# A 3x3 convolution inside a fused network: nine taps, or minimal filtering over pairs of columns

## The chip, the cores and the metric

The kernel runs as one program on one core of a Trainium2 chip. The metric is the device time of one execution in microseconds (us). Engines are named as the profile names them: PE (TensorE matmul), PEld (TensorE weight load), DVE (VectorE), ACT (ScalarE), POOL (GpSimd) and SP (SyncE, which here only issues DMAs). The time before the change is 3184.22 us, the median of three runs (3183.93 to 3184.84).

## The reference

The input is `x`, two images of 128 channels and 56 x 56 pixels in float32. Four layers follow, each added to `x` after a normalization of its input: agent attention (L0), a 3x3 convolution with 128 channels in and out (L1), a mixture of 8 experts over 2x2 patches with the two best experts for each patch (L2), and a two-way state space scan over rows (L3). The reference writes the convolution with Fourier transforms; what it computes is

```python
PAD = 1
xp = jnp.pad(x, ...)                       # one pixel of zeros on every side
out = sum over i, j of weight[:, :, i, j] applied to xp[:, :, i : i + 56, j : j + 56]
return out + bias[None, :, None, None]
```

which is nine products of a 128 x 128 matrix with shifted pictures.

## The kernel before, in words

`layers` (line 1864) runs the four layers in order. Channels lie on the 128 partitions and pixels on the free axis; an image of 3136 pixels is worked on in seven blocks of 448 columns (8 rows), `BLK`, `NBLK` and `ROWS`. `x` stays in SBUF for the whole kernel, and each layer adds its result to it in place. After each such addition `take_stats` (line 84) takes the statistics of the block, and `group_norm` (line 90) later turns the seven into mean and inverse deviation, which takes two tiny matmuls and two ACT operations. `normed` (line 109) applies them.

**Attention.** `short_attention` (line 384) goes through 14 blocks (7 of each image), each in 25 steps. In every step, `score` (line 574) makes scores on PE and exponentials on ACT and sums them on DVE (lines 592 and 594), and `average` (line 596) multiplies an earlier step's exponentials with the values. The exponentials have five buffers. The order of PE, ACT and DVE is written out by hand there (`manual_schedule`, line 732); POOL is not among these engines and is ordered by the framework's planner, which works with its own estimates of cost. At set steps the loop also runs a piece of other work: the pieces that close the block before (`after`, line 720: divide, project, measure, root, normalize, turn_back, restat), those that prepare the next one (`ahead`, line 729), and at the free steps whatever stands in the list `rest`: first image 0's last values, the preparation of the convolution's weights (`taps`, line 441) and the opening of image 1. POOL does two things here: the softmax scaling of `a_e` (line 549) and the addition of a finished block to `x` (line 687).

**Convolution of image 0.** It is begun in the attention. From the last but one block on (line 744), `rest` holds the norm of image 0 and seven calls of `pad` (line 846), which write normalized rows into a picture with a border of zeros, 58 x 58, in the buffer that held image 0's normalized input. After the last block, at line 784, the seven closing pieces of that block alternate with seven calls of `block` (line 864): nine matmuls of 448 columns into one PSUM bank, one for each tap, then one DVE operation that adds bias and result to `x` (line 876), then the statistics. A check of the softmax's ranges follows (lines 793 to 812); its one number `wide` decides at the end of the kernel whether everything is done again with `agent_attention`. In the profile it isn't.

**Convolution of image 1.** It lies in the routing of the experts. `route` (line 900) calls `convolved` (line 1879) for each image; image 0 is already done, and for image 1 it takes the norm, pads the whole picture with `pad` on DVE into a buffer of the experts' weights (tag `w1`), and then gives out one block at a time. After the second block the router's work for image 0, `patches(0)` (line 962), is issued; after the last one, that for image 1. Then follow the routing tables, the gathers, and the experts. At the same time `MambaWeights` (line 1300) loads the weights of the last layer through ACT's DMA queue and turns them with PE and DVE. In this part the planner orders all engines.

**Weights.** `loads` (line 828) fetches the 128 x 128 x 9 weights and turns them with nine PE transposes in three calls of `turn`, each followed by one ACT copy into `wt`.

[...]in the attention three pairs for scores and passing work (tag `sc`) and two single ones; in the convolution of image 1 four banks for its sums (tag `conv`).

## Time and profile before

| what | us |
|---|---|
| median of the three timed runs | 3184.22 |
| the profiled execution's own time | 3175.44 |
| its span, first to last instruction | 3173.7 |
| attention ends (last softmax sums on PE) | about 902 |
| convolution of image 0 on PE | 901.9 to 953.0 |
| range check, norm of image 1 | 953.0 to 963.5 |
| convolution of image 1 on PE, with image 0's router work | 964.1 to 1019.6 |
| routing | 1020 to 1068 |
| experts | 1068 to 1749 |
| last layer | 1749 to 3174 |

One execution was profiled, so all durations below come from it; the median is of other executions. A row of a stretch gives its length and the busy time of each engine in it, with the count of instructions in brackets. A row of the timeline gives start, length, engine, line, operation and how many like instructions were merged; what stands in square brackets is the idle time of the engine ahead of it and what ended it. A row of a tile or a line gives the least, median and greatest duration in nanoseconds. A float32 matmul leaves two records, so counts of matmul records are twice the counts in the code.

### The profile page before, as it was taken

How to read it: one execution, taken by the hardware profiler on the slowest of the kernel's cores; microseconds unless marked ns; L12 is line 12 of the kernel's file. 1: busy time of each engine (PE TensorE's matmuls, PEld its weight loads, DVE VectorE, ACT ScalarE, POOL GpSimd, SP SyncE). 2: the span in 40 equal slices, each digit the busy share in tenths (PEclk: the TensorE clock that was granted, in tenths of full speed). 3: DMA queues.
4: the chain of work that ended last, by engine and by line, in shares of the span. 5: the costliest groups of instructions: out<-in, count | busy, mean ns of one | idle time of the engine just before them, and what ended most of it. 6: DMA issues, size and time to landing. Idle time of an engine off the chain costs nothing. (4 is left out here: it accounts for less than half of the span.)

```text
span 3173.7 us, 34586 instructions
## 1 busy us (share of the span) xinstructions
PE 2863.2 (90%) x13024; PEld 1091.1 (34%) x13024; DVE 2201.9 (69%) x1985; ACT 1752.3 (55%) x2618; POOL 1411.1 (44%) x755
## 2 busy tenths in 40 slices
PE   7899999998999799999995689998898988999985
PEld 3233333332344444444442223332233332233321
DVE  5788999998854211111112389999999999999997
ACT  5678878887720111111100367777777777777764
POOL 2000010000000000000002389999999999999996
PEclk9999999999998899999997698998999999898987
DMA  1000000000001687878755434454444354445350
GB/s 53 1 1 1 1 1 1 1 1 1 1 31 27 266 323 283 324 282 322 286 228 178 103 72 95 88 104 89 92 87 101 84 107 89 85 87 108 81 111 7
DMA packets 133397, 333.65 MB, mean 105 GB/s; under 512 B 20100, under 2 KB 90596, under 8 KB 129620
## 3 DMA queue, kind: packets, MB, share of 16 engines
q1 hardware_dynamic: 111616, 304.87, 33.5%
q0 software_dynamic: 5136, 14.70, 1.4%
q10 hardware_dynamic: 16452, 11.61, 1.1%
q8 instruction: 107, 1.75, 0.2%
q14 instruction: 86, 0.70, 0.1%
HBM read 262.56 MB, written 17.20 MB: 88 GB/s over the span
## 5 line engine op out<-in xcount | busy, mean ns | idle before, releaser
L1667 POOL TENSOR_TENSOR dBu<-dtu,Bs 128x896 f32<-128x896 f32 x448 | 923.2, 2087 | 72.2 <-DVE h L1689 52.2
L1689 DVE TENSOR_TENSOR_SCAN h<-dA,dBu 128x896 f32<-128x896 f32 x448 | 878.6, 2006 | 58.1 <-ACT dA L1656 56.5
L587 ACT ACTIVATE ex<-sc 128x896 f32<-128x896 f32 (+1 forms) x700 | 602.8, 917 | 111.1 <-PE sc L584 99.9
L594 DVE TENSOR_TENSOR ex_sum<-ex_sum,ex 128x1792 f32<-128x1792 f32 (+1 forms) x238 | 490.0, 2059 | 44.1 <-ACT ex L587 30.0
L1709 PE MATMUL y<-h,both 128*64 128x448 f32 x1792 | 474.5, 631 | 15.6 <-POOL h L1695 13.0
L584 PE MATMUL sc<-q,k 32*128 32x448 f32 (+1 forms) x2800 | 403.0, 589 | 3.6 <-ACT ex L587 2.9
L1208 PE MATMUL h_ps<-w,xs_c 128*128 128x512 f32 x896 | 392.0, 595 | 10.6 <-issue 9.9
L1656 ACT ACTIVATE dA<-dt,f_A 128x448 f32<-128x448 f32 x448 | 284.4, 637 | 110.3 <-DVE h L1689 76.8
L602 PE MATMUL av<-ex,va 128*32 128x448 f32 (+1 forms) x2800 | 335.0, 553 | 0.1
L1698 DVE TENSOR_TENSOR h<-h,c_ps 128x1792 f32<-128x1792 f32 x154 | 311.3, 2022 | 25.6 <-PE c_ps L1677 10.8
L549 POOL TENSOR_TENSOR a_e<-a_e,a_inv 112x784 f32<-112x784 f32 x14 | 41.6, 2973 | 644.1 <-ACT ex L587 436.5
L1656 ACT ACTIVATE dA<-dt,b_A 128x448 f32<-128x448 f32 x448 | 283.7, 636 | 62.9 <-DVE h L1689 50.0
L1212 DVE TENSOR_TENSOR he<-h_ps,sg 128x512 f32<-128x512 f32 x56 | 38.6, 691 | 397.0 <-PE h_ps L1208 374.3
L1159 POOL DMA_INDIRECT xr<-xd,whom x28 | 28.0, 998 | 593.8 <-PE xr_ps L1198 489.2
L1695 POOL TENSOR_TENSOR h<-h,Cs 128x1792 f32<-128x1792 f32 x70 | 279.1, 3986 | 3.2 <-DVE h L1689 2.8
L1677 PE MATMUL c_ps<-low,ident 40*64 40x448 f32 x616 | 173.2, 643 | 91.4 <-DVE h L1698 69.3
L1208 PEld LDWEIGHTS h_ps<-w,xs_c 128*128 128x128 f32 x896 | 168.5, 190 | 218.6 <-issue 201.9
L1709 PEld LDWEIGHTS y<-h,both 128*64 128x64 f32 x1792 | 117.9, 152 | 319.9 <-issue 248.4
L584 PEld LDWEIGHTS sc<-q,k 32*128 32x128 f32 (+1 forms) x2800 | 137.4, 181 | 231.1 <-issue 134.8
L1229 PE MATMUL o_ps<-w,ht 128*128 128x512 f32 x448 | 200.0, 599 | 8.0 <-DMA w<-in_L_conv_w_dram 8.0
L1231 ACT ACTIVATE ot<-o_ps,share 128x512 f32<-128x512 f32 x28 | 19.2, 688 | 287.0 <-PE o_ps L1229 287.0
L1211 ACT ACTIVATE sg<-h_ps 128x512 f32<-128x512 f32 x56 | 33.4, 597 | 256.8 <-PE h_ps L1208 256.8
(318 smaller groups left out, 3007.1 us busy)
## 6 DMA issues: line engine op xcount, KB each, us to landing
w<-in_L_conv_w_dram SPq DMA_DIRECT2D x28, 4096.0 KB, 19.5
w<-in_L_conv_w_dram SPq DMA_DIRECT2D x28, 2048.0 KB, 10.3
Bs<-far SPq DMA_DIRECT2D x56, 896.0 KB, 10.7
dtu<-sp_u SPq DMA_DIRECT2D x112, 224.0 KB, 3.9
dt<-dt SPq DMA_DIRECT2D x112, 224.0 KB, 5.2
Cs<-far SPq DMA_DIRECT2D x140, 112.0 KB, 7.5
os<-ot ACTq DMA_DIRECT2D x28, 256.0 KB, 7.8
xd<-xt SPq DMA_DIRECT2D x14, 224.0 KB, 2.8
```

Of the source, the lines that this page charges most:

```text
L584: nc.tensor.matmul(sc[:size, j, :BLK], self.m.k[rows, at : at + size], self.q[rows, :], start=True, stop=True)
L587: nc.scalar.activation(ex[:size, 2 * g : 2 * g + 2, :], sc[:size, :, :BLK], AF.Exp, scale=scale)
L594: nc.vector.tensor_add(self.total[g][:size], self.total[g][:size], ex[:size])
L602: nc.tensor.matmul(self.av[rows, :BLK], self.m.va[:size, i, rows], self.ex[i][:size, h, :], start=i == 0, stop=i == STEPS - 1,)
L1208: nc.tensor.matmul(h_ps, xc[:, q, :], w1[:, q, f0 : f0 + 512], start=q == 0, stop=q == 3)
L1229: nc.tensor.matmul(o_ps, ht[:, i, :], w2[:, i, :], start=i == 0, stop=i == nj - 1)
L1656: nc.scalar.activation(self.dA[u][:, r * BLK : (r + 1) * BLK], self.dt2[:, m, r, :], AF.Exp, scale=self.w.A[:, j, 2 * m + r : 2 * m + r + 1],)
L1667: nc.gpsimd.tensor_tensor(self.dBu[u], self.dtu2[:, m], self.B[:, j, :].unsqueeze(1).to_broadcast(shape), ALU.mult)
L1689: nc.vector.tensor_tensor_scan(hf, af, bf, 0.0, ALU.mult, ALU.add)
L1695: nc.gpsimd.tensor_tensor(h4, h4, c, ALU.mult)
L1698: nc.vector.tensor_tensor(h4, h4, c, ALU.mult)
L1709: nc.tensor.matmul(self.y[r * H : (r + 1) * H, m, :BLK], both, self.hc[j][:, m, r, :], start=False, stop=j == PAIRS - 1)
```

## The change

Two neighbouring outputs of a row need four neighbouring padded columns d0, d1, d2, d3. With the taps k0, k1, k2 of a row of the filter the change forms four products in place of six: k0 (d0 - d2), (k0 + k1 + k2)/2 (d1 + d2), (k0 - k1 + k2)/2 (d2 - d1) and k2 (d1 - d3). The first output is the first product plus the second plus the third; the second output is the second minus the third minus the fourth. Summed over the three rows of the filter this is twelve products for each pair of columns, each over half as many columns.

- `loads` keeps nine transposes, now grouped by column of the filter, three to a copy, and gets a fourth stage, `mix`, of four POOL operations that forms the two mixed sets. `wt` grows from 9 to 12 matrices.
- `pad` becomes `planes`: the normalized rows go into a small scratch buffer with two places (8 rows of 58 each), and four two-input operations over every second column write four planes of 28 columns. For image 0, inside the attention, these run on POOL; for image 1 on DVE. The planes of image 0 lie in the former buffers of its input and its keys (`xn0`, `k0`), the scratch in that of its values (`va0`); those of image 1 in a `w1` and a `w2` buffer of the experts.
- `block` becomes `group`: 16 rows at a time (three groups, and one of 8 rows), in halves. `left` makes products 1 and 2 (six matmuls into two banks), adds the first to the even columns of `x` on DVE, and copies the second, with bias, to SBUF on ACT. `right` makes products 3 and 4, copies the third with ACT, and subtracts the fourth from the odd columns on DVE. `rest` forms difference and sum of the two copies on POOL, adds them on DVE and takes the statistics of the group's blocks. A group's `rest` is issued behind the next group's `left`.
- In the tail of the attention the seven closing pieces alternate with eight half groups. In the routing, `patches(0)` is issued after the first group in place of the second block. The sums have two pairs of banks in place of four single ones.

```diff
-                    pad = one.tile([P, PAD * PAD], F32, name="pad0", tag="xn0")
+                    planes = [
+                        one.tile([P, PAD * PAD], F32, name=f"planes{i}", tag=tag)[:, : PAD * HW].rearrange(
+                            "c (i h w) -> c i h w", i=2, h=PAD
+                        )
+                        for i, tag in enumerate(("xn0", "k0"))
+                    ]
+                    scratch = one.tile([P, len(tiles), P], F32, name="scratch", tag="va0")
+                    scratch = scratch.rearrange("p n d -> p (n d)")[:, : conv.SCRATCH]
                     rest = [lambda: conv.norm(0, banks, "mm")]
-                    rest += [lambda k=k: conv.pad(0, pad, k) for k in range(NBLK)]
+                    rest += [lambda k=k: conv.planes(0, planes, k, scratch, nc.gpsimd) for k in range(NBLK)]
...
-            for k in range(NBLK):
-                if k < len(tail) and tail[k]:
-                    fetch = tail[k]()
-                conv.block(0, k, pad, bank("conv_ps"))
-                if k < len(tail) and tail[k] and fetch:
-                    fetch()
+            parts, end = [], None
+            for g in range(len(conv.GROUPS)):
+                left, right, finish = conv.group(
+                    0, g, planes, scratch, lambda name: ps.tile([P, 2, 512], F32, name=name, tag="sc")
+                )
+                parts += [(left, end), (right, None)]
+                end = finish
+            for n, (part, ready) in enumerate(parts):
+                fetch = tail[n]() if n < len(tail) else None
+                part()
+                if fetch:
+                    fetch()
+                if ready:
+                    ready()
+            end()
...
+    HALF = HW // 2
+
+    GROUPS = ((0, 16), (16, 16), (32, 16), (48, 8))
+    SCRATCH = 2 * ROWS * PAD + 5 * BLK
...
+        def mix():
+            k0, k1, both, k2 = (self.wt[:, :, n, :] for n in range(4))
+            nc.gpsimd.tensor_tensor(both, k0, k2, ALU.add)
+            nc.gpsimd.tensor_tensor(k1, k1, both, ALU.add)
+            nc.gpsimd.tensor_scalar(k1, k1, 0.5, 0.0, ALU.mult, ALU.add)
+            nc.gpsimd.tensor_tensor(both, both, k1, ALU.subtract)
...
+    def planes(self, b, planes, k, scratch, engine):
 
         nc = self.net.nc
+        half = self.HALF
+        at = k % 2 * ROWS * PAD
+        p3 = scratch[:, at : at + ROWS * PAD].rearrange("c (h w) -> c h w", w=PAD)
+        nc.gpsimd.memset(p3[:, :, :: PAD - 1], 0.0)
         self.net.normed(
+            p3[:, :, 1 : PAD - 1], self.net.xb(b, k).rearrange("c (h w) -> c h w", w=HW), self.norms[b]
         )
+        even, odd = (p3.rearrange("c h (w two) -> c h two w", two=2)[:, :, i, :] for i in range(2))
+        rows = slice(1 + k * ROWS, 1 + (k + 1) * ROWS)
+        for n, (left, right, op) in enumerate(
+            (
+                (even[:, :, :half], even[:, :, 1:], ALU.subtract),
+                (odd[:, :, :half], even[:, :, 1:], ALU.add),
+                (even[:, :, 1:], odd[:, :, :half], ALU.subtract),
+                (odd[:, :, :half], odd[:, :, 1:], ALU.subtract),
+            )
+        ):
+            engine.tensor_tensor(planes[n // 2][:, n % 2, rows, :], left, right, op)
+        for edge in [0] * (k == 0) + [PAD - 1] * (k == NBLK - 1):
+            for two in planes:
+                nc.gpsimd.memset(two[:, :, edge, :], 0.0)
+
+    def group(self, b, g, planes, scratch, banks):
+
         net, nc = self.net, self.net.nc
+        r0, rows = self.GROUPS[g]
+        half = self.HALF
+        n = rows * half
+        x = net.x[:, b, r0 * HW : (r0 + rows) * HW].rearrange("c (h w two) -> c two h w", two=2, w=half)
+        at = 2 * ROWS * PAD
+        first, second, gap = (
+            scratch[:, at + i * BLK : at + i * BLK + n] for i in (g % 2 * 2, g % 2 * 2 + 1, 4)
+        )
...
+        def products(two):
+            m = banks("conv_ps")
+            for i in range(2):
+                for row in range(3):
+                    nc.tensor.matmul(
+                        m[:, i, :n],
+                        self.wt[:, row, 2 * two + i, :],
+                        planes[two][:, i, r0 + row : r0 + row + rows, :].rearrange("c h w -> c (h w)"),
+                        start=row == 0,
+                        stop=row == 2,
+                    )
+            return m
+
+        def left():
+            m = products(0)
+            nc.vector.tensor_tensor(x[:, 0], x[:, 0], grid(m[:, 0, :n]), ALU.add)
+            nc.scalar.activation(first, m[:, 1, :n], AF.Identity, bias=self.bias, scale=1.0)
+
+        def right():
+            m = products(1)
+            nc.scalar.copy(second, m[:, 0, :n])
+            nc.vector.tensor_tensor(x[:, 1], x[:, 1], grid(m[:, 1, :n]), ALU.subtract)
+
+        def rest():
+            nc.gpsimd.tensor_tensor(gap, first, second, ALU.subtract)
+            nc.gpsimd.tensor_tensor(first, first, second, ALU.add)
+
+            nc.vector.tensor_tensor(x[:, 1], x[:, 1], grid(gap), ALU.add)
+            nc.vector.tensor_tensor(x[:, 0], x[:, 0], grid(first), ALU.add)
+            for k in range(r0 // ROWS, (r0 + rows) // ROWS):
+                net.take_stats(b, k)
+
+        return left, right, rest
...
-                if k == 1:
+                if k == 0:
                     patches(0)
...
                         conv.norm(b, ps, "mm")
                         for k in range(NBLK):
-                            conv.pad(b, pad, k)
-                        for k in range(NBLK):
-                            conv.block(b, k, pad, ps.tile([P, 512], F32, name="conv_ps", tag="conv", bufs=4))
-                            yield k
+                            conv.planes(b, planes, k, scratch, net.nc.vector)
+                        end = None
+                        for g in range(len(conv.GROUPS)):
+                            left, right, finish = conv.group(
+                                b,
+                                g,
+                                planes,
+                                scratch,
+                                lambda name: ps.tile([P, 2, 512], F32, name=name, tag="conv", bufs=2),
+                            )
+                            left()
+                            if end:
+                                end()
+                            right()
+                            end = finish
+                            yield g
+                        end()
```

Besides, the fallback attention has one `a_en` buffer in place of two, and the buffers `k0`, `k1` and `cw` take the size of the padded picture.

## The prediction

> **What bounds the kernel now.** I read the page first, then busy time by stretch, then the waits and the order of time between 902 and 1068 us, where the convolution lies. The page's chain of waits only covers the last 60 us and says nothing of it.
>
> ```profile
> span 3173.7 us, 34586 instructions
> PE 2863.2 (90%) x13024; PEld 1091.1 (34%) x13024; DVE 2201.9 (69%) x1985; ACT 1752.3 (55%) x2618; POOL 1411.1 (44%) x755
> ```
>
> TensorE (PE) is the busiest engine over the whole span. By stretch (columns: length, then busy time of PE, weight load, DVE, ACT, POOL, then PE clock, DMA share, GB/s):
>
> ```profile
> 800.00:862.00 62.00, 61.66 (x500) 20.11 (x498) 55.61 (x51) 50.33 (x63) 4.95 (x2) 1.00 0.00 1
> 902.00:954.00 52.00, 51.04 (x138) 25.77 (x138) 20.59 (x51) 1.82 (x4) 5.46 (x24) 0.96 0.16 47
> 964.00:1020.00 56.00, 55.98 (x187) 29.32 (x186) 17.77 (x49) 5.11 (x10) 0.00 (x0) 0.97 0.10 29
> ```
>
> The second and third rows are the convolutions of image 0 and image 1: PE is full, ACT and POOL nearly idle. The first row is the attention block in which image 0's padded copy is written: DVE and PE are both near full, POOL idle. Of the waits in 902 to 1068, the largest that matters is the evacuation waiting for PE:
>
> ```profile
> DVE x L876 <- PE conv_ps L869: 63.1, 14, 6.3
> PE w_ps L811 <- DVE bad_sum L809: 4.7, 1, 4.7
> ```
>
> PE in order of time (start, length, merged records):
>
> ```profile
> 901.88 9.29 PE L869 MATMUL conv_ps<-pad,cwt 128*128 128x448 f32 x18
> 911.88 27.23 PE L869 MATMUL conv_ps<-pad,cwt 128*128 128x448 f32 x72
> 964.14 15.63 PE L869 MATMUL conv_ps<-pad,cwt 128*128 128x448 f32 x36
> ```
>
> A matmul leaves two records (252 for 126), so at speed one costs 2 x 27.23/72 = 0.756 us; 63 of them, 47.6 us an image. The first row is slow (18 records take 9.29, at speed 6.81): 2.5 us of slow start, and 2.0 in the third (15.63 against 13.6). Between the two convolutions DVE shows the joint:
>
> ```profile
> 953.80 0.63 DVE L88 BATCH_NORM_STATS2 st<-x 128x6 f32<-128x448 f32 x1
> 957.21 0.18 DVE L1367 TENSOR_SCALAR f_A<-f_A 128x32 f32<-128x32 f32 x1 [1.35 <-ACT f_A L1366]
> 958.01 0.14 DVE L812 TENSOR_SCALAR wide<-w_ps 1x1 int32<-1x1 f32 x1 [0.37 <-PE w_ps L811]
> 963.54 3.04 DVE L110 TENSOR_SCALAR pad<-x,gn_mean,gn_rstd 128x448 f32<-128x448 f32 x7
> 1019.83 0.69 DVE L876 SCALAR_TENSOR_TENSOR x<-conv_ps,c_L_conv_bias,x 128x448 f32<-128x448 f32 x1 [5.42 <-PE conv_ps L869]
> ```
>
> So: conv of image 0, range check until 958.0, norm of image 1, pads at 963.5, conv of image 1 at 964.1 to 1019.6, its last evacuation, then router norm and routing. Each waits for the one before; all of it is on the path to the experts at 1068.
>
> [...]
>
> ```profile
> L687 POOL TENSOR_TENSOR x<-x,z x14: 1129/1680/2527, 162.8 to 940.4; 128x448 f32<-128x448 f32 x14
> L549 POOL TENSOR_TENSOR a_e<-a_e,a_inv x14: 1499/3086/3088, 33.2 to 816.6; 112x784 f32<-112x784 f32 x14
> L1280 DVE TENSOR_TENSOR x<-x,y_ps x56: 214/266/273, 1723.7 to 1763.7; 128x112 f32<-128x112 f32 x56
> ```
>
> The first two double between least and most. [...] No POOL row here shows a step. [...]
>
> **The change, part by part.**
>
> *Matmuls.* Per image 63 of 448 columns go; three groups of 12 at 448 columns and one of 12 at 224 come. 36 x 0.756 + 12 x 0.378 = 31.8 us against 47.6: 15.8 less, twice. A 224-column record would be 0.19; transposes of 112 columns run at 0.55/4 = 0.14 (turn_back, L681), so loads allow it. Bound: 0.19 to 0.26 a record, at most 1.7 us more an image. I take 0.19.
>
> *Image 0's planes, in the attention.* Seven DVE normalizations stay (0.51 each). POOL gets 28 subtractions or adds of 224 elements, plus memsets at 0.11. Price from L687 and L549 scaled to 224: 0.43 to 1.26; I take 1.0, being beside a busy DVE. 28 us of POOL lie in a block where POOL now works 4.95 of 62 us. Added wait: normalization k writes the scratch slot that POOL's k-2 read, so DVE waits for POOL; behind it stand the adds of L594, and behind those the `ex` buffers (five), ACT and PE. By the times of L110 (799.6, 802.1, 821.1, 823.5, 830.9, 833.2, 838.9), at 4.1 us for each k POOL ends k2 at 825.7, k3 at 829.8, then z's add at 831.7, k4 at 835.8: every slot is free in time and restat (836.4) too. Cost 0, up to 2 us at 1.26. Were the cover gone, it is the slower rival below.
>
> *Weights.* Nine transposes and three ACT copies stay; a fourth step (mix) puts four POOL operations of 384 elements, about 1 to 2 us each, into block 0, where POOL's next work is a_e some steps later. 0.
>
> *Image 0's groups.* Eight half groups replace seven blocks, tail steps between them. PE: 31.8 + 2.5 + 1.6 (project 1.04, turn_back 0.55), so it ends at 901.9 + 35.9 = 937.8 instead of 953.0. ACT's copy of y now stands behind the copy of the first right half (about 914), so measure starts near 914.5, before the left half of group 1 is out; the chain measure, root, normalize (1.9 + 0.6 + 1.6) still precedes turn_back. z's POOL add comes at about 935. After the last matmul: ACT copy and DVE subtract 0.4, two POOL operations 1.3 (behind group 2's two at 1.13, done near 938), two DVE adds 0.7, statistics 0.6: about 3.5 us against 1.4 now. Statistics end near 941.7. The check took 3.7 us, 1.35 of it waiting for f_A, whose load is issued by ACT's queue from 941.6 on; if it isn't in front, the check takes 2.6 and ends at 945 (958.1 before): **13 us gained**.
>
> *Image 1's planes.* Norm chain as before, 5.4 us. Then DVE builds planes: 0.43 + 4 x 0.31 = 1.7 us each (issue intervals; a dense add of n elements is about 0.16 + n x 1.03 ns long, from 448 and 1792 elements at 0.63 and 2.02; it starts 0.09 before the last one ends). Group 0 needs three of them: 5.0 us before the first matmul against 0.6. Loses 4.4: PE starts at 955.5, 8.6 ahead. L1280 shows stepped adds at the dense price; bound 0.63 each, another 4 us.
>
> *Image 1's groups.* PE: 55.5 becomes 31.8 + 2.1 slow start + 5.8 for image 0's router products: 39.7. DVE has all seven planes first (11.8 us), so the first left half waits for its evacuation and, with two PSUM pairs, PE loses about 1.5. Then DVE has per group 2 x 0.68 + 2 x 0.63 + 2 x 0.63 = 3.9 us against 9.1 of PE. PE ends near 996.8 (1019.6). End chain 1.8 longer than now. **Sum: 8.6 + 15.8 - 1.5 - 1.8 = 21.** Evacuation on ACT and POOL (about 0.6 and 1.1 to 2.5) lies under PE. Routing and experts shift unchanged: the second buffer of `w2` goes to the room, the first to scratch, both free before the loads (the second w1 load waits for the same product, L1145, at 1059.0). The fallback attention does not run: 0.
>
> The profiled run took 3175.4 (span 3173.7 plus 1.7), the three timed runs 3184.2; the 8.8 between is no part of these stages, so I subtract from the median: 3184.2 - 21 = **3163**.
>
> **Rivals.** *DVE bounds image 1's stage.* For: planes, weights and evacuations together are some 40 us, near PE's 40; the planner may put weight copies in front. Against: dense prices leave it slack. At 0.63 for stepped adds of 224 and 1.1 of 448, DVE needs about 50 us after the norm: 3173. *The last stage's weight loads set the joint.* [...]f_A (957.2) and b_scaled wait for loads that start only when the attention's buffers are free. If they stay ahead of the check or the planes, PE starts at 964 as now: 21 - 8.6 = 12.4 gained, 3172. Against: in 969 to 1019 they weren't late. *Slower: POOL holds DVE in the attention.* At price c, POOL ends k4 at 821.6 + 12c + 1.9, DVE wants it at 838.9: stall 12c - 15.4. It eats the 21 us from c = 3.0 on; at c = 4, 32.6 lost, 3184 + 12 = 3196. Against: 3.0 is over twice the dearest price shown. For: no row has POOL reading steps.
>
> **Numbers.** Forecast 0.62, with its own range 3154 to 3170 (planner luck, slow starts, stepped prices); DVE bound 0.15; loads 0.13; POOL 0.10. Range 3154 to 3178: leaves out POOL's case and the tails of two others. A change under 0.2% (6.4 us) can't be told from none here. Faster 0.82 (the first three less 0.08 for their tails), same 0.08, slower 0.10.
>
> **What would show it.** Conv matmul records 192 instead of 252, busy near 34 us an image; wide (L812 before) near 945; image 1's first conv matmul near 955; its last near 997; attention's end still 902. Wrong if conv matmuls of 224 columns cost as much as 448, if PE waits for DVE over 4 us in image 1's stage, if the attention ends after 905, or if POOL's plane operations take over 1.3 us.

## The result, and the profile after

The changed kernel takes 3169.25 us (median of 5 runs, 3163.07 to 3170.24); the kernel before took 3184.38 us in the same series (5 runs, 3183.93 to 3185.91). The ratio is 0.9945, 95% interval 0.993 to 0.996: 15 us saved, where 21 were forecast. A later series of the same two kernels gave 3167.83 (4 runs) against 3186.42 (8 runs), 0.9942 (0.9921 to 0.9964), 18.6 us. So the sign and the order of size are as forecast; the question is which steps of the sum held.

The page of the profile after (the profiled execution took 3169.25 us):

```profile
span 3167.5 us, 34586 instructions
PE 2842.5 (90%) x12964; PEld 1081.8 (34%) x12964; DVE 2223.2 (70%) x2031; ACT 1760.5 (56%) x2634; POOL 1480.7 (47%) x793
```

PE is 20.7 us less busy than before (30.6 in the second pair of profiles below), DVE 21.3 us and POOL 69.6 us more. Busy shares don't say where the end moved, so I lay the two traces side by side by landmarks. By stretch (length, then busy time of PE, weight load, DVE, ACT, POOL, PE clock, DMA share, GB/s), the convolution of image 0, the joint, and the convolution of image 1:

```profile
907.50:941.50 34.00, 33.97 (x112) 19.71 (x108) 18.38 (x35) 5.01 (x10) 8.67 (x8) 0.98 0.00 0
941.50:957.40 15.90, 3.60 (x14) 2.56 (x14) 12.58 (x55) 1.50 (x6) 5.68 (x32) 0.66 0.51 154
957.40:999.30 41.90, 41.79 (x155) 23.92 (x156) 26.11 (x72) 8.84 (x17) 8.86 (x10) 0.96 0.25 50
```

From first to last matmul, the two stretches in which PE is full shrank from 51.2 to 34.0 and from 55.6 to 42.1 us; the joint, in which it mostly stands still, grew from 11.1 to 15.9. The products by shape (busy, mean ns of a record, idle before):

```profile
L922 PE MATMUL conv_ps<-planes,cwt 128*128 128x448 f32 x144 | 59.0, 560 | 2.1 <-POOL scratch L884 2.0
L922 PE MATMUL conv_ps<-planes,cwt 128*128 128x224 f32 x48 | 9.4, 352 | 0.0
```

192 records in place of 252, as the prediction wanted. (The records overlap: the 144 have a mean of 560 ns, where the run of 48 below has one every 379 ns. So the price is read from the length of a run of records.) Image 0's last two runs:

```profile
913.81 18.20 PE L922 MATMUL conv_ps<-planes,cwt 128*128 128x448 f32 x48
932.24 9.23 PE L922 MATMUL conv_ps<-planes,cwt 128*128 128x448 f32 x36
```

The first is 0.379 us a record. The second holds 12 records of 448 columns, 4.55 us at that price, and 24 of 224 columns in the remaining 4.68: 0.195 each, half. All landmarks, with the gain of each step over the kernel before (from unrounded times; `wide` is the number that the range check writes):

| from ... to | before | after | gain | predicted |
|---|---|---|---|---|
| block 11's `att` copy to first convolution matmul | 125.5 | 129.2 | -3.7 | 0 |
| first matmul of image 0 to `wide` | 56.1 | 42.5 | +13.6 | +13.0 |
| `wide` to first matmul of image 1 | 6.1 | 7.3 | -1.2 | -4.4 |
| image 1's matmuls | 55.6 | 42.1 | +13.6 | +14.2 |
| last matmul to the statistics' sum (L94) | 1.6 | 3.5 | -1.9 | -1.8 |
| L94 to the first expert matmul | 47.1 | 48.8 | -1.6 | 0 |
| sum up to the experts | | | 18.8 | 21.0 |
| first expert matmul to the combine's first gather | 647.2 | 648.5 | -1.2 | 0 |

That leaves 17.6 us at the combine, between the 15.1 and the 18.6 of the two series. What the table leaves out differs between single executions of one kernel; three places have it. In the opening, block 2's `att` copy stood at +1.90 us against the kernel before in this profile, +0.99 in a second one of the same kernel, and -1.04 in a second one of the kernel before. Behind the first gather, DVE stands still with no releaser that the profile knows. The same instruction in the first and the second profile of the kernel before, and in the changed one:

```profile
1744.97 0.16 DVE L66 TENSOR_SCALAR ir_v<-gn_ps 128x1 f32<-128x1 f32 x1 [0.50 <-PE gn_ps L104]
```

```profile
1749.01 0.16 DVE L66 TENSOR_SCALAR ir_v<-gn_ps 128x1 f32<-128x1 f32 x1 [4.78 <-remote]
```

```profile
1735.46 0.16 DVE L66 TENSOR_SCALAR ir_v<-gn_ps 128x1 f32<-128x1 f32 x1 [4.72 <-remote]
```

And the last layer, from its first convolution matmul to the end, takes 1424.0 us in the first profile of the kernel before and 1430.1 in the second (1427.3 and 1427.4 in the two of the changed kernel). The first profile of the kernel before happened to be without the stall and with the shorter last layer (3175.4 us, where its timed runs are at 3181 to 3193), so the difference of the first two profiles' ends, 6 us, must not be read as the change's worth.

**Where 3.7 us went in the attention.** Blocks 12 and 13, before and then after (columns as above):

```profile
776.37:844.77 68.40, 60.15 (x473) 19.94 (x468) 57.51 (x60) 47.52 (x62) 4.95 (x2) 0.93 0.00 1
844.77:898.71 53.94, 53.12 (x433) 15.55 (x428) 50.51 (x43) 43.33 (x54) 1.75 (x1) 1.00 0.01 1
```

```profile
778.29:847.02 68.73, 60.47 (x473) 20.15 (x468) 57.29 (x58) 47.51 (x61) 34.51 (x30) 0.93 0.00 1
847.02:904.37 57.35, 53.34 (x433) 15.45 (x428) 55.45 (x45) 43.34 (x55) 14.41 (x7) 1.00 0.01 1
```

POOL's busy time went from 6.7 to 48.9 us, DVE's from 108.0 to 112.7 though it issues no operation more: both slowed each other. The plane operations by engine (least/median/most ns), and DVE's normalization in the attention (busy, mean ns):

```profile
L898 POOL TENSOR_TENSOR planes<-scratch x28: 554/2234/2346, 802.1 to 857.4; 128x224 f32<-128x224 f32 x28
L898 DVE TENSOR_TENSOR planes<-scratch x28: 384/385/389, 955.7 to 966.9; 128x224 f32<-128x224 f32 x28
```

```profile
L110 DVE TENSOR_SCALAR scratch<-x,gn_mean,gn_rstd 128x448 f32<-128x448 f32 x7 | 5.3, 762 | 1.8 <-POOL scratch L884 1.8
```

On POOL the same 224 elements take 0.55 us at best, 2.23 at the median and 1.55 on average; beside them DVE's normalizations take 0.76 in place of 0.51, and its sums of exponentials (L594) 2.11 on average in place of 2.07. The order of time shows when an operation is dear. The last of these four on POOL begins at 842.16, while a sum runs on DVE, and ends at 844.50, 0.4 us after that sum:

```profile
838.66 5.84 POOL L898 TENSOR_TENSOR planes<-scratch 128x224 f32<-128x224 f32 x4
841.72 2.37 DVE L594 TENSOR_TENSOR ex_sum<-ex_sum,ex 128x1792 f32<-128x1792 f32 x1
```

So it is with all 15 operations, of the 28, that begin while DVE sums exponentials (L592 or L594): they take 2.19 to 2.35 us and end 0.42 to 0.43 us after the sum. The other 13 take 0.55 to 1.01. What DVE loses shows in PE. Two products of block 13 that waited for nothing in the kernel before wait for DVE in the changed one:

```profile
847.91 0.94 PE L622 MATMUL den<-ex_sum,full 128*32 128x448 f32 x8
857.30 1.10 PE L641 MATMUL y_ps<-wpt,att 128*112 128x128 f32 x8
```

```profile
852.41 0.96 PE L622 MATMUL den<-ex_sum,full 128*32 128x448 f32 x8 [2.06 <-DVE ex_sum L594]
862.94 1.10 PE L641 MATMUL y_ps<-wpt,att 128*112 128x128 f32 x8 [1.24 <-DVE att L633]
```

PE stands idle for 3.96 us in block 13 in place of 0.78. That is 3.2 of the 3.4 us by which the block grew.

**Image 0's tail**, from 937 us (start, length):

```profile
937.40 0.73 ACT L685 ACTIVATE z<-z_ps,c_L_conv_ln_b,c_L_conv_ln_g 128x448 f32<-128x448 f32 x1
937.58 1.15 POOL L942 TENSOR_TENSOR scratch<-scratch 128x448 f32<-128x448 f32 x1 [7.07 <-ACT scratch L938]
938.80 1.13 POOL L943 TENSOR_TENSOR scratch<-scratch 128x448 f32<-128x448 f32 x1
939.89 1.13 POOL L687 TENSOR_TENSOR x<-x,z 128x448 f32<-128x448 f32 x1
941.05 0.63 DVE L88 BATCH_NORM_STATS2 st<-x 128x6 f32<-128x448 f32 x1 [2.90 <-POOL x L687]
...
946.72 0.39 DVE L946 TENSOR_TENSOR x<-x,scratch 128x224 f32<-128x224 f32 x1 [0.55 <-POOL scratch L943]
```

z's addition stands behind group 2's pair on POOL and ends at 941.0, DVE waits 2.90 us for it, and everything of group 3 is behind that wait. The prediction had z's addition ahead of that pair, at about 935; but z itself leaves ACT only at 938.1, behind the copy of group 2's right half. The tail takes 8.6 us from the last matmul (941.5) to `wide` (950.0), where 7.2 were predicted. PE itself was 2.0 us faster than predicted, mostly because its slow start was shorter: its first 12 records take 5.58 us, 1.0 over the price at speed, where 2.5 were reckoned.

### The profile page after: what moved, and what is told of

The parts are those of the page before. It is cut to its first block, busy times and chain, and to the rows that moved or that the text cites. A ratio compares the mean times of both kernels' runs of the same rounds, so it can differ in the third digit from the quotient of the medians.

```text
span 3167.5 us, 34586 instructions
## 1 busy us (share of the span) xinstructions
PE 2842.5 (90%) x12964; PEld 1081.8 (34%) x12964; DVE 2223.2 (70%) x2031; ACT 1760.5 (56%) x2634; POOL 1480.7 (47%) x793
## 5 line engine op out<-in xcount | busy, mean ns | idle before, releaser
L594 DVE TENSOR_TENSOR ex_sum<-ex_sum,ex 128x1792 f32<-128x1792 f32 (+1 forms) x238 | 492.2, 2068 | 44.4 <-ACT ex L587 30.4
L584 PE MATMUL sc<-q,k 32*128 32x448 f32 (+1 forms) x2800 | 404.5, 592 | 3.6 <-ACT ex L587 2.9
L549 POOL TENSOR_TENSOR a_e<-a_e,a_inv 112x784 f32<-112x784 f32 x14 | 41.6, 2974 | 543.0 <-ACT ex L587 392.6
L584 PEld LDWEIGHTS sc<-q,k 32*128 32x128 f32 (+1 forms) x2800 | 137.8, 183 | 232.3 <-issue 136.7
```

What stands on the lines that cost most here:

```text
L584: nc.tensor.matmul(sc[:size, j, :BLK], self.m.k[rows, at : at + size], self.q[rows, :], start=True, stop=True)
L594: nc.vector.tensor_add(self.total[g][:size], self.total[g][:size], ex[:size])
```

## The experiments

My theory after the first comparison: the matmuls are worth what was predicted, and what is missing was lost in three places, two of which the sum held at nothing: 1.9 us early in the attention (the extra weight stage), 3.7 us in blocks 12 and 13 (POOL's plane operations), and the rest in the order of image 0's tail. Rivals: stepped reads are what POOL pays for; DVE simply has no room; the early loss is noise.

**c_after**: the changed kernel once more. **c_before**: the kernel before once more.

> The changed kernel once more, as the measure for the three edits beside it. Same stage times as in its first profile: block 2 of the attention 1.9 us behind the kernel before, first convolution matmul at 907.5 us (5.6 behind), second image's convolution 41.9 us long. If the 6 us by which the executions of either kernel differ among themselves lie in the experts' combine, as the first pair of profiles suggests (waits there that no semaphore explains), the two profiles of this one kernel may differ there and nowhere else. Time 3163 to 3170.

> The kernel before once more, for a second profile. Its profiled execution took 3175.4 us and its timed ones 3181 to 3193; the three profiles of kernels of the new form so far all spend 39.4 to 40.0 us from the first gather of the combine to the last layer's first convolution, where the first profile of the kernel before spent 34.0. If that stall moves from execution to execution, this profile shows 39 to 40 us there too, with about 3181 us or more in all. If it belongs to the new program, this profile shows 34.0 again. Block 2 of the attention may stand up to 2 us off the first profile either way: the four profiles of programs with the same opening spread over 2.7 us there.

c_after: 3167.83 us. First convolution matmul 906.61, block 2 at +0.99 us; blocks 12 and 13 together 126.08 us, as in the first profile. c_before: 3185.61 us; 40.1 us from the first gather to the last layer's first convolution (34.0 in its first profile); blocks 12 and 13 together 122.32 (122.34 at first). So the stall behind the gather is no property of the change: of the fourteen profiles in this study thirteen have 39 to 41 us there, and only the very first of the kernel before has 34. The length of a block repeats to 0.05 us, which makes it the measure for all that follows. What I expected of the opening's spread held. That two profiles of one kernel would differ in the combine alone did not: they differ by 0.9 us in the opening too, and those of the kernel before by 6.1 us in the last layer.

**e1_mix_step**: the mixed weights without a stage of their own.

```diff
-            return lambda: nc.scalar.copy(
-                self.wt[:, :, plane, :], ps[:, : 3 * P].rearrange("c (i f) -> c i f", i=3)
-            )
+            def fetch():
+                nc.scalar.copy(
+                    self.wt[:, :, plane, :], ps[:, : 3 * P].rearrange("c (i f) -> c i f", i=3)
+                )
+                if plane == 3:
+                    mix()
+            return fetch
...
-        return [lambda at=at: turn(*at) for at in ((0, 0), (1, 1), (2, 3))] + [mix]
+        return [lambda at=at: turn(*at) for at in ((0, 0), (1, 1), (2, 3))]
```

> The four GpSimd operations that make the mixed weights are issued right behind the copy of the third column's turned weights, and not as a stage of their own, so that the stages which open the second image stand where they stood before. Theory (the added stage moves the opening of image 1 by one step and so costs the 1.9 us that are already lost at block 2): from block 2 to block 11 the attention is within 0.5 us of the kernel before, the first convolution matmul comes at about 905.6, the time falls by 1.9 us. Rival (the four GpSimd operations themselves, 8.3 us, slow the engines beside them in block 0): the 1.9 us stay, and the time with them.

3166.60 us, 0.9939 (0.9917 to 0.9961). After block 0 it stands at +0.64 where the change stands at -3.2 to -4.1, so the stage does move the opening; but from block 2 on it is at +0.95, inside the -1.41 to +1.90 that the other profiles with the changed opening show. The early 1.9 us of the first profile lie within what single executions differ by, and the stage costs nothing that can be seen: this part of the theory falls.

**e2_planes_dve** and **e3_dense**: image 0's planes on DVE; and dense reads in place of stepped ones.

```diff
-                    rest += [lambda k=k: conv.planes(0, planes, k, scratch, nc.gpsimd) for k in range(NBLK)]
+                    rest += [lambda k=k: conv.planes(0, planes, k, scratch, nc.vector) for k in range(NBLK)]
```

```diff
-            p3[:, :, 1 : PAD - 1], self.net.xb(b, k).rearrange("c (h w) -> c h w", w=HW), self.norms[b]
+            p3.rearrange("c h (two w) -> c h two w", two=2)[:, :, :, :half],
+            self.net.xb(b, k).rearrange("c (h w two) -> c h two w", two=2, w=half),
+            self.norms[b],
...
-        even, odd = (p3.rearrange("c h (w two) -> c h two w", two=2)[:, :, i, :] for i in range(2))
+        odd, even = p3[:, :, : half + 1], p3[:, :, half + 1 : 2 * half + 2]
```

> The sums of columns of the first image on VectorE in place of GpSimd: 28 operations of 0.385 us (the price of the same line in the second image), 10.8 us in blocks 12 and 13, where VectorE had some 15 us free in the kernel before. Theory (GpSimd's 2.2 us operations cost the 3.7 us of these blocks, by slowing VectorE and by holding the scratch ring): VectorE's sums of exponentials stay at about 2.0 us each, the first convolution matmul comes at 904 to 906 in place of 907.5, time 1.5 to 3.5 us less. Rival (VectorE sets these two blocks): the 10.8 us come on top for the most part, first convolution matmul at 910 or later, time 3 us more or worse.

> The normalization writes odd and even columns of a row side by side, so that the 28 operations on GpSimd (and the 28 on VectorE for the second image) read runs of 28 elements in place of every second element; all else as in the change. Theory (the stepped read is what makes them dear beside a busy VectorE): from 2.23 us to 1.0 to 1.3 us each, the 3.7 us of blocks 12 and 13 shrink to about 1.5, first convolution matmul at about 905.3. Rival (any GpSimd operation beside VectorE's two-operand sums pays this): still about 2.2 us each, first convolution matmul at 907.5, time as the change. On VectorE 0.385 us either way.

e2: 3166.13 us, 0.9943 (0.9925 to 0.9961). Blocks 12 and 13:

```profile
776.35:846.78 70.43, 60.47 (x473) 19.87 (x468) 62.68 (x86) 47.52 (x62) 6.37 (x7) 0.93 0.00 1
846.78:902.81 56.03, 53.33 (x432) 15.45 (x428) 54.12 (x45) 43.34 (x54) 1.73 (x1) 1.00 0.01 1
```

DVE's sums are back at 2.07 us and its normalizations at 0.51, the 28 operations take 0.39 each, and the two blocks are 126.46 us long: 4.1 lost, not less than with POOL. The first convolution matmul, at 905.21, falls where the theory wanted it (904 to 906), but for the most part because this execution's opening was earlier; relative to block 11 it comes only 0.4 us earlier than in the change. The rival's 910 is missed too. e3: 3165.88 us, 0.9936 (0.9914 to 0.9958), blocks 126.54 us, and

```profile
L902 POOL TENSOR_TENSOR planes<-scratch x28: 557/2224/2381, 799.4 to 855.1; 128x224 f32<-128x224 f32 x28
```

The rival holds: stepped or dense, POOL pays 2.2 us (medians of 2.23 and 2.22). And taking the operations off POOL doesn't help: 28 sums of columns in these two blocks cost about 4 us wherever they run. On DVE they add 8.8 us to its busy time; on POOL, in 42.6 us of work, they make DVE 4.7 us busier and let it wait 1.8 us for `scratch`. No run separates that slowing from that waiting.

**e6_no_planes0**: none of the 28.

```diff
-                    rest += [lambda k=k: conv.planes(0, planes, k, scratch, nc.gpsimd) for k in range(NBLK)]
+                    planes[1] = planes[0]
+                    rest += [lambda k=k: conv.planes(0, planes, k, scratch, None) for k in range(NBLK)]
...
+        if engine is None:
+            flat = planes[0].rearrange("c i h w -> c (i h w)").rearrange("c (h w) -> c h w", w=HW)
+            self.net.normed(
+                flat[:, 1 + k * ROWS : 1 + (k + 1) * ROWS, :],
+                self.net.xb(b, k).rearrange("c (h w) -> c h w", w=HW),
+                self.norms[b],
+            )
...
+            return
```

> The 28 sums of columns of the first image are left out: the normalization writes rows of 56 straight to the first pair of planes, and all products of the first image read that pair. So what it computes for image 0 is another thing; only its time counts. Theory (blocks 12 and 13 have no room for these operations on any engine that shares VectorE's work: 3.7 us lost with them on GpSimd, 3.3 with them on VectorE): from block 11 to the first convolution matmul it is within 0.7 us of the kernel before. Rival (another edit costs it, such as the single buffer of the normalized agent weights): 2 us or more stay.

One run, 3158.07 us. Blocks 12 and 13:

```profile
776.89:845.79 68.90, 60.65 (x473) 20.15 (x468) 57.50 (x60) 47.49 (x61) 4.96 (x2) 0.93 0.00 1
845.79:899.75 53.96, 53.13 (x434) 15.55 (x428) 50.51 (x43) 43.33 (x55) 1.74 (x1) 1.00 0.01 1
```

122.86 us, 0.5 over the kernel before, and from block 11 to the first convolution matmul 126.01 in place of 125.50: the theory holds. 3.2 of the 3.7 us are the plane operations, with the memsets and the ring of scratch slots that go with them and are left out too. The dose goes on upwards by an oversight of mine in e10 and e11 (below): there 14 of image 0's 28 operations are issued a second time, and in e10 the two blocks take 130.61 us (DVE's wait for `scratch` grows as well, from 1.8 to 5.0 us).

| operations in blocks 12 and 13 | none (before, e6) | 28 on POOL (change, e1, e3, e5) | 28 on DVE (e2) | 42 on POOL (e10) |
|---|---|---|---|---|
| length of the two, us | 122.3, 122.9 | 126.1 to 126.5 | 126.5 | 130.6 |

**e5_tail**: the tail's order.

```diff
-                part()
                 if fetch:
                     fetch()
+                part()
-            nc.gpsimd.tensor_tensor(gap, first, second, ALU.subtract)
-            nc.gpsimd.tensor_tensor(first, first, second, ALU.add)
+            engine = nc.vector if g >= 2 else nc.gpsimd
+            engine.tensor_tensor(gap, first, second, ALU.subtract)
+            engine.tensor_tensor(first, first, second, ALU.add)
```

> Two edits to the order behind the products: in the first image's tail each stage's copy is issued ahead of the products' evacuation, so that the last attention block's addition on GpSimd does not stand behind the sums of the third group; and the sum and difference of the products of the third and fourth groups go to VectorE (both images). Theory (the order and GpSimd's queue cost the tail 2 to 3 us): from the end of the first image's matmuls to the check 5.5 to 6.5 us in place of 8.6, from the end of the second image's matmuls to the statistics' sum 2.5 to 3.5 us in place of 3.5, time 2 to 3.5 us less than the change. Rival (VectorE's own work sets the tail): 8 us or more, time as the change.

3165.09 us, 0.9939 (0.9922 to 0.9955), no different from the change. From the last matmul of image 0 to `wide` it is 6.4 us (theory: 5.5 to 6.5), so the diagnosis of the tail is right; the two edits were not tried apart. But PE's stage became 1.5 us longer (35.4), so first matmul to `wide` gains 0.7. That is not the tail's doing: the first 12 records of the convolution are slow, as they are in e1, which has no edit there. In the change, in e1 and in e5, behind the same stop of PE of 1.55 us:

```profile
907.52 5.58 PE L922 MATMUL conv_ps<-planes,cwt 128*128 128x448 f32 x12
```

```profile
906.58 7.08 PE L928 MATMUL conv_ps<-planes,cwt 128*128 128x448 f32 x12
```

```profile
904.18 7.05 PE L922 MATMUL conv_ps<-planes,cwt 128*128 128x448 f32 x12
```

Then image 1 starts 8.1 us after `wide` in place of 7.3: the planner has put seven copies of the last layer's weights (L117) into the norm's chain there, where the change has one. Its matmuls take 44.7 us in place of 42.1; 1.4 of that is again a slow start (7.49 us to the thirteenth record in place of 6.07; PE's clock over the first 8 us is 0.63 in place of 0.81), 0.6 a wait for DVE (`xq`, L110), the rest I didn't find. The end chain is 3.1 (theory 2.5 to 3.5, in place of 3.5), and the experts start 46.6 us after it in place of 48.8. Relative to block 11 the first expert matmul is 0.2 us later than in the change. The 2 us that the tail had to give are there, and the total doesn't show them; 2.9 us of slow starts of PE lie against them, and whether the edits bring these on, no run here says.

**e7_spread**, **e9_norm8**, **e8_two**: where the planes stand. All three issue the norm at step 19 of block 8 (image 0 is complete after block 7).

```diff
-                if n == len(blocks) - 2:
+                if n == 8:
-                    elif rest and (i > 2 or n == 0):
+                    elif rest and ((n, i) in slots if n >= 8 else i > 2 or n == 0):
```

with `slots` for e7 and for e8, and in e9 another condition, by which all steps of planes stay in blocks 12 and 13:

```diff
+            slots = [(8, 19), (8, 22), (9, 22), (10, 22), (11, 22), (12, 22), (13, 5), (13, 22)]
```

```diff
+            slots = [(8, 19), (8, 22), (9, 7), (9, 22), (10, 7), (10, 22), (11, 7), (11, 22)]
```

```diff
+                    elif rest and ((n, i) == (8, 19) if 8 <= n < 12 else i > 2 or n == 0):
```

> The first image's norm and its seven steps of planes start in block 8 and go one to a block up to block 13, in place of all in blocks 12 and 13; same operations on the same engines. Theory (blocks 12 and 13 are crowded, while a block of 58.6 us leaves VectorE 5.2 us): the lost 3.7 us fall to 0 to 1.5, first convolution matmul 2 to 3.7 us earlier relative to block 7 than in the change, time less by as much. Rival (each step costs PE its half us wherever it stands, because PE fills 99% of a block and waits for the slowed VectorE): the same 3.7 us, spread over six blocks.

> Of the spread version only the move of the norm: it stands in block 8, the seven steps of planes stay in blocks 12 and 13. The spread version came out 6.3 us ahead of the change at the first convolution matmul. Theory (two separate gains: the norm is cheaper in block 8 by some 4 us, and the planes cost 3.7 us where they crowd blocks 12 and 13): the first convolution matmul is 2.5 to 4.5 us earlier than in the change relative to block 7, and blocks 12 and 13 together still lose 2.5 to 4 us. Rival (norm and planes together made the crowd): all 6.3 us are there with the norm moved alone.

> The first image's norm and first step of planes in block 8 as in the spread version, the other six steps two to a block in blocks 9 to 11, none in 12 and 13. Theory (a block of 58.6 us has 5.2 us free on VectorE, and two steps cost it some 2 normalizations of 0.75 us and about 3 us of slower sums): blocks 9 to 11 stay within 0.5 us of 58.6 each, and the 1.0 us that block 13 still lost in the spread version goes, so that the first convolution matmul is 0.5 to 1.0 us earlier than there, relative to block 7. Rival (two in a block are too many): 0.5 us or more lost in each of the three blocks, nothing gained.

e7: 3158.72 us, 0.9918 (0.9895 to 0.9941). Block 8, a middle one, and blocks 12 and 13:

```profile
542.17:606.61 64.44, 61.44 (x473) 19.86 (x468) 55.06 (x54) 47.50 (x62) 7.77 (x4) 0.95 0.01 1
606.61:665.19 58.58, 57.91 (x468) 18.75 (x464) 54.14 (x46) 47.09 (x60) 10.50 (x8) 1.00 0.00 1
782.36:840.94 58.58, 57.92 (x469) 18.76 (x464) 54.16 (x46) 47.09 (x60) 10.52 (x8) 1.00 0.00 1
840.94:895.87 54.93, 53.82 (x433) 15.55 (x428) 52.18 (x45) 43.23 (x55) 12.73 (x11) 1.00 0.01 1
```

A block with one step of planes is 58.58 us long, as without: the cost is nothing at all, and PE keeps its 57.9 us. Only block 13 with its two steps loses 1.0, and PE's stop ahead of the convolution is 1.96 us in place of 1.55. The first convolution matmul is 6.3 us earlier than in the change relative to block 7, more than the theory wanted. e9 asks how much of it is the norm. One run, 3164.10 us; blocks 8, 12 and 13:

```profile
542.02:606.46 64.44, 61.44 (x472) 19.87 (x468) 54.96 (x53) 47.55 (x62) 4.76 (x2) 0.95 0.01 1
782.24:844.39 62.15, 59.03 (x469) 18.76 (x464) 56.99 (x50) 47.15 (x60) 43.20 (x32) 1.00 0.00 1
844.39:902.03 57.64, 54.92 (x433) 15.68 (x428) 54.79 (x45) 43.37 (x54) 9.33 (x5) 0.97 0.01 1
```

Both expectations miss: the norm moved alone brings 0.8 us. The norm costs 64.44 - 58.58 = 5.9 us in block 8 (9.8 in block 12 of the kernel before, with seven normalizations). But the steps of planes, seven normalizations among them, now with no norm's stall of PE to lie under, cost 62.15 - 58.58 + 57.64 - 53.94 = 7.3 us; some 1.5 of that is PE at about half speed behind a stop of 1.59 us in block 13 (the row's clock is 0.97 in place of 1.00; eight records of L622 take 1.66 us there in place of 0.96, eight of L584 1.87 in place of 1.03). That the change hid part of this cost under the 7.2 us that PE stands still for the norm in block 12 is what the difference suggests; no run shows it directly. So crowding costs 7.3 us here and spreading takes all but 1.0 of it away: by the end of block 13 e7 is 6.3 us ahead of e9.

e8: 3157.01 us, 0.9915 (0.9898 to 0.9933), 28 us under the kernel before in its series; by time it can't be told from e7, whose runs go from 3150.62 to 3165.70. Blocks 8 and 9:

```profile
541.83:603.39 61.56, 58.56 (x473) 19.29 (x468) 54.95 (x54) 47.51 (x62) 7.76 (x4) 1.00 0.01 1
603.39:662.51 59.12, 58.05 (x468) 18.65 (x464) 55.18 (x47) 47.09 (x60) 15.40 (x13) 1.00 0.00 1
```

Two steps in a block cost 0.54 us, three times (0.39 of it one stop of PE for `a_e` of POOL, L549, which e7's blocks don't have; what makes `a_e` late there I didn't follow), and blocks 12 and 13 lose 0.4 (58.58 and 54.30): 2.0 us in all against e7's 1.0, or 1.4 with its longer stop ahead of the convolution. So the rival is right, and one step to a block is the better rule. That e8 is still 1.9 us ahead of e7 by the end of block 13 (3.1 at the first convolution matmul, where the theory wanted 0.5 to 1.0) lies in block 8 (61.56 against 64.44), and that is PE's clock after the norm (the block's rows show 1.00 in e8 and 0.95 in e7). The rest lies ahead of the convolution: e8's eight records of L622 take 0.96 us there and e7's 1.72, and e7's stop is longer (1.96 us against 1.56). The end of this text has more on it.

**e10_order1** and **e11_best**: image 1's planes in another order; and that with e8.

```diff
-                        for k in range(NBLK):
-                            conv.planes(b, planes, k, scratch, net.nc.vector)
+                        for ks in ((0, 1, 2), (3, 4), (5, 6)):
+                            later = [conv.planes(b, planes, k, scratch, net.nc.vector, 3) for k in ks]
+                            for late in later:
+                                late()
...
+        make(0)
+        if bands == 2:
+            make(1)
...
+        return lambda: make(1)
```

> In the second image VectorE makes the first pair of planes of the first three bands ahead of their second pair (then bands 3 and 4, then 5 and 6, likewise), because the first six matmuls read the first pair alone. Theory (three bands' planes stand between the check and PE): the six operations put behind, 6 times 0.385 = 2.3 us, come off the 7.3 us between the check and the first matmul of image 1, and the norm after this image comes 1.5 to 2.3 us earlier. Rival (PE then waits for the second pair, or VectorE's evacuation stands behind the later planes): the start is 2.3 us earlier, the end of the stage within 0.5 us of where it was.

> Norm in block 8 with the planes two to a block, and the second image's planes in the new order, together. Theory: the gains add, 6.3 to 7.3 us at the first convolution matmul of image 0 and 1.5 to 2.3 us in image 1, some 8 to 9.5 us less than the change: ratio to the kernel before 0.9910 to 0.9920. Rival (what is gained ahead of the experts is taken by the stage behind it, as 1.6 us are now): under 6 us less than the change.

Here `make(0)` and `make(1)` are the two operations of the first and of the second pair, and scratch has three slots for image 1. In both kernels the returned function also ran for image 0, whose second pair was so made twice (the 14 extra operations above); that wasn't meant and spoils their totals: 3168.68 us, 0.9944 (0.9927 to 0.9961), and 3161.38 us, 0.9925 (0.9910 to 0.9940). (e11's first convolution matmul is 6.8 us earlier than in the change relative to block 7, as its theory wanted.) It gives one more point of the dose: in blocks 9 to 11 four such operations (e7) cost 0.00 us a block, eight (e8) 0.54, twelve (e11) 1.09. Image 1's stage can be read by itself. In e10 from `wide` to the first matmul it is 6.7 us, 0.6 earlier and not 2.3: in the change PE had begun after two bands already (a group of 16 rows needs the third only for its lowest row of taps). And from `wide` to L94 it is 56.0 us in place of 52.9. The first evacuation, in the change and in e10:

```profile
965.42 0.62 DVE L933 TENSOR_TENSOR x<-x,conv_ps 128x448 f32<-128x448 f32 x1
```

```profile
967.44 0.63 DVE L940 TENSOR_TENSOR x<-x,conv_ps 128x448 f32<-128x448 f32 x1
```

It comes 15.4 us after `wide` in the change (950.04) and 16.2 in e10 (951.22), where all planes stand ahead of it. PE, with two pairs of PSUM banks, then stands idle for 1.32 us until the second pair is read, later for 0.57 (`xq`) and 1.30 us (`xt`), none of which the change has, and its start is 0.6 us slower (its first 24 records take 11.36 us in place of 10.74); that makes up the longer stage. How much of it the order of the planes brings on, with ACT's queue full of loads until 968.5, I didn't separate. The theory's gain isn't there; the rival had PE's wait right, but neither its early start nor its end.

## Why the prediction was nearly right

**The mechanism held**: in each image 63 products of 448 columns became 36 of 448 and 12 of 224, worth 42, and the 224-column record was worth half, as taken. At the plain price that is 15.8 us a stage. PE's stage in image 0 shrank by 17.2, of which 1.5 are a shorter slow start; image 1's shrank by 13.6 (14.2 predicted, with 1.5 of waiting). Image 0 from first matmul to `wide` gained 13.6 (13.0 predicted).

**The step that failed is "Image 0's planes, in the attention: Cost 0, up to 2 us".** It measured 3.7 us, and two of the prediction's own signs of being wrong came: the attention ended after 905 (first convolution matmul at 907.5, of which 1.9 belong to the opening), and POOL's plane operations took over 1.3 us. Two things were wrong in the step. The price: 1.0 us was taken, with 1.26 as the upper end, scaled from operations of 448 and 784 elements; it was 1.55 on average and 2.23 at the median. The dear part is the time until DVE's sum is over, up to 1.92 us (2.35 less 0.43), and a price scaled by width has no term for it; what does grow with the width is the part behind the sum, 0.42 us at 224 elements, 1.00 at 448 (L687) and 1.35 at 784 (L549). With 1.55, the prediction's own formula, 12c - 15.4, gives 3.2 us of stall. And the reasoning: it followed the ring of two scratch slots and asked when a slot is free, and so what DVE *waits* for POOL (1.8 us in all). It didn't ask what POOL does to DVE's own durations, though the row of a_e shows the effect from POOL's side: 1.50 us in the one execution with no sum of DVE beside it, 3.08 to 3.09 in the 13 others. DVE lost 4.7 us of busy time with no operation more. e2 shows that the place is short of DVE time in either case, e6 that nothing else costs more than 0.5 us there, e7 that the same operations cost nothing in blocks with 5.2 us of DVE free and one step each. The "slower" rival had the right place and the right engine, and the price at which it would have decided (3.0 us an operation) was not reached.

**Image 1's start** was mis-sized the other way: 7.3 us from the check to the first matmul where 10.5 were reckoned, because the sum let group 0 wait for three bands and PE needs two to begin (2.5 us from the first normalization to PE, where 5.0 were reckoned), and the norm's chain was 4.8 us in place of 5.4. That gave back 3.2 us and hid most of the attention's loss. That the total came so near is in part luck: this error and PE's faster start happened to stand against the losses.

**The tail** was sized at 7.2 us and took 8.6: the order on POOL was assumed (z's addition ahead of group 2's pair) and was the other way round, with z itself late from ACT. PE's shorter slow start made up for it. The prediction had carried the slow start over from the trace of the kernel before as a fixed 2.5 us. It isn't fixed: PE's stop ahead of the convolution is 1.55 us, before and after, and the slow start behind it was 2.5 us in the one and 1.0 in the other (granted clock over the first 5.1 us: 0.55 and 0.84).

**The experts' start and the combine** were held at nothing and lost 1.6 and 1.2 us: the weight copies and the second transfer of the first expert's rows may now come closer to the path (ahead of the first expert matmul PE waits 1.17 us for the second `xr`, where it waited 0.33). No run isolates these.

**The rivals**: DVE bound in image 1 (no: 26.1 us busy of 41.9), weight loads at the joint (no: the first matmul came 7.3 us after the check; but ACT stood 6.2 us idle ahead of its first evacuation of image 1, with eight loads being issued on its queue), POOL in the attention (in part).

## What to carry to other kernels

An operation put on an idle POOL beside a busy DVE wasn't free here: POOL took 2.19 to 2.35 us beside a sum of DVE where it takes 0.55 at best, and DVE's own instructions became 4.7 us longer. So price that slowing, not only DVE's waits for the result. Small work that has no deadline belongs one piece to a block into the slack of many blocks (0.00 us each in e7), not into the last two before it is needed (3.7 us in the change, 7.3 in e9). When the profiles of two kernels are compared, take lengths between landmarks that repeat (a block repeated to 0.05 us), and profile the kernel before twice before any difference of ends is believed.

## What was not expected of the hardware

- PE's clock after a short stop. In e7, e9, e8 and e11, PE stands idle for 1.54 and 0.79 us around the norm's two small products in block 8. In e7 and e9 the next products run at about half speed for some 7 us (8 records of L584 in 1.87 us; granted clock of the block 0.95); in e8 and e11 they run at full speed at once (1.03 us; 1.00). The idle times are the same to 0.01 us. This is worth 2.9 us (64.44 against 61.56). Ahead of image 0's convolution it is the same: behind a stop of 1.55 us the stage takes 33.1 us in e2, e3 and e10, 34.0 in the change and 35.4 in e1 and e11, with the same matmuls; the two kernels profiled twice repeat it to 0.02 us. Nothing in the traces says what decides it, so a difference of 2 to 3 us behind such a stop can't be put down to an edit.

```profile
590.89 1.87 PE L584 MATMUL sc<-q,k 32*128 32x448 f32 x8
```

```profile
590.34 1.03 PE L584 MATMUL sc<-q,k 32*128 32x448 f32 x8
```

- A sum of 224 elements on POOL spreads from 0.55 to 2.35 us, a factor of four: all 15 that begin while DVE runs a two-input sum of 1792 elements end 0.42 to 0.43 us after that sum, and the other 13 take at most 1.01. DVE needs 0.39 us for such a sum of 224.
- The stall of 4.7 us on DVE among the combine's gathers, with no releaser in the profile, which one of two profiles of the same program lacked.
